# First attention of a four-stage block: ScalarE and VectorE take the order of the source

## The chip, the cores and the metric

One core of a Trainium2 chip runs the whole program. The core has five engines with a queue each: TensorE (PE: matrix products; PEld is its weight load), VectorE (DVE), ScalarE (ACT), GpSimd (POOL) and SyncE (SP, which issues most DMAs). An engine takes its queue in order: an instruction that waits for a semaphore holds up all behind it. Matrix products write to PSUM, eight banks of 128 partitions by 512 fp32 numbers. The metric is the device time of one execution in microseconds (us), as the median of three runs.

## The reference

The input x is 4 sequences (batches) of 512 tokens with 512 channels. Four layers are added to it in turn, each of a normed x: an attention, a feed-forward with ternary weights, a state-space scan and an attention with a mixture of experts. The change lies in the first, cut here to what is computed (16 heads of 32 channels; queries and keys are rotated, then divided by their root mean square, and the softmax is causal):

```python
def attention0(x, W_qkv, W_o):                 # x: (4, 512, 512), layer-normed
    qkv = einsum('btc,oc->bto', x, W_qkv).reshape(B, T, 3, 16, 32)
    q, k, v = (transpose(qkv[:, :, i], (0, 2, 1, 3)) for i in range(3))
    q = rms_norm(q * cos + rotate_half(q) * sin)
    k = rms_norm(k * cos + rotate_half(k) * sin)
    scores = where(causal, einsum('bhqd,bhkd->bhqk', q, k) / sqrt(32), -1e9)
    out = einsum('bhqk,bhkd->bhqd', softmax(scores), v)
    return out.transpose(0, 2, 1, 3).reshape(B, T, C) @ W_o.T

def ternary_quant(w):                          # for w1, w3 (1365 x 512) and w2 (512 x 1365)
    s = mean(abs(w))
    return clip(round(w / s), -1, 1) * s
```

The ternary weights are needed only in the second layer. The kernel prepares w1 and w3, and the scale of w2, while the first attention runs.

## The kernel before

**Order.** The program is written with a scheduler that works out each engine's order at compile time from a cost model, hands out buffers, and places all semaphores. The first attention stands in a block in which TensorE is ordered by hand, that is, as the source has it (`tc.manual_schedule(engines={mybir.EngineType.PE})`). VectorE, ScalarE and GpSimd are ordered by the scheduler there, so an instruction of a later line may pass one of an earlier line where the cost model expects it to be ready sooner.

**Buffers.** Four PSUM banks (`bank`) serve everything of one bank: projections `pq`, transposes `tp`, the products `av` and `sm`, the output projection `y`, and `sp`. A new one waits until the last reader of the bank's former tile is through. The other four banks are two pairs (`pair`) for the scores. Normed rows (`row`) have two buffers, as have rotations and their squares (one tag, `rot`), and the raw weight pieces (`q_w`).

**Prologue.** Batch 0 is normed (`norm`: statistics of four row tiles of 128 tokens, the factor by a power on GpSimd, L102 and L103). `turn_in` makes each normed row (L123, VectorE), transposes it on TensorE (L132) and copies it to `hT` on ScalarE (L133). `project(b, t, s)` (L284) computes queries (s=0), keys (1) or values (2) of row tile t. For queries and keys it then rotates: two products with the sine (L296) and one with the cosine (L300) on VectorE, their sum on GpSimd (L303), the square on ScalarE (L305), the sum of squares on VectorE (L306). Values are copied by ScalarE (L289). `scale_heads(b, i)` works out 1/rms for two row tiles by eleven short VectorE instructions (L312 to L323) and scales the heads (L325, two of 128x1024). `turn_heads(b, t)` transposes queries and keys (L132) and ScalarE copies them to `qkT` (L133). At the end of the prologue batch 1 is normed and its rows are transposed.

**Batches.** `attend(b, between)` goes through 16 steps m, four groups of four heads by four key tiles j. A step computes scores of 128 keys against the 512 - 128 j queries that see them (L359, two PSUM pairs of two heads), their exponentials on ScalarE (`pt`, L364, one instruction for each pair), and the causal cut on GpSimd (L365). Then it runs what `between[m]` holds, and last `weigh` of the step before: products with the values and with ones (`av` and `sm`, L377). After the fourth key tile of a group come VectorE's reciprocal of the sums (L385, 3.36 us) and the product with it (`oT`, L386).

`between` weaves other work in: `back` of the batch before (steps 1 to 4; output projection L340, sum L343), the projections of the next batch (step 0 and steps 5 to 15, in the order (0,0), (0,1), (1,0), (1,1), (0,2), (2,0), (2,1), (1,2), (3,0), (3,1), (2,2), (3,2) of (t, s)), `scale_heads` at 9 and 14, `turn_heads` at 12 and 13, and the weight pieces. After the last step follow `turn_heads` for tiles 2 and 3, and `norm` and `turn_in` of the batch after the next.

**Weight pieces.** `jobs` is a list of 43 pieces, each fetched by SyncE into `q_w` (L218); the end of a piece's job issues the load two places on. Eight pieces of w1 are measured in batch 0 (ScalarE: absolute value with a running sum, L234), eight quantized in batch 1 (VectorE, L201 and L202) in turn with pieces of w2 that are measured (L252). Batch 2 measures the last of w2 and w3, batch 3 quantizes w3. `find_scale` turns a weight's measured sums into its scale: `ternary_scale` sums them on VectorE (L187), adds up the partitions on TensorE (`sp`, L189) and makes three constants on VectorE (L193).

Of the kernel before, what the change touches and what calls it, by code (L numbers as in the profile page):

```python
# [19 lines left out]
P = 128  # L20
# [26 lines left out]
def block_kernel(ctx: ExitStack, tc: tile.TileContext, a: dict, out: bass.AP):  # L47
# [116 lines left out]
    with tc.tile_pool(name="a_w", bufs=1) as aw, tc.tile_pool(name="a_1", bufs=1) as a1, tc.tile_pool(  # L164
# [19 lines left out]
        def ternary_scale(pool, parts, name):  # L184

            tot = pool.tile([P, 1], F32, tag="q_tot", name="q_tot")
            nc.vector.tensor_reduce(tot, parts, AX.X, ALU.add)  # L187
# [68 lines left out]
        def find_scale(name):  # L256
            scales[name] = ternary_scale(a1, parts[name], name)
# [6 lines left out]
        normed, inputs_T, heads, squares, turned_qk, values, outs = {}, {}, {}, {}, {}, {}, {}  # L264

        def norm(b, pieces=1):
            normed[b] = []
            layer_norm(a1, xs[b], lambda t, op: normed[b].append(op), pieces)
            inputs_T[b] = a1.tile([P, NK, T], F32, tag="hT", name="hT")
# [4 lines left out]

        def turn_in(b, i):
            for t in (2 * i, 2 * i + 1):
                row = a2.tile([P, C], F32, tag="row", name="row")
                normed[b][t](row)
                transpose_into(inputs_T[b], row, t * P)
# [120 lines left out]
        with tc.manual_schedule(engines={mybir.EngineType.PE}):  # L400

            norm(0, 2)
            for i in range(2):
                turn_in(0, i)
                for t in (2 * i, 2 * i + 1):
                    project(0, t, 0)
                    project(0, t, 1)
                scale_heads(0, i)
# [5 lines left out]
            norm(1)  # L414
# [25 lines left out]
            for b in range(B):  # L440
# [1364 lines left out]
```

## Time and profile before

| | |
|---|---|
| Median of 3 runs | 1862.88 us (1862.3 to 1863.4) |
| The profiled execution | 1863.49 us, of which the span from first to last instruction is 1861.8 |
| PE busy | 1757.1 us, 94% of the span |
| DVE, ACT, POOL busy | 1123.3 (60%), 938.3 (50%), 568.4 us (31%) |
| Prologue, to the first scores | 0 to 63.4 us |
| Batch 0, 1, 2 (first scores to next first scores) | 88.0, 112.0, 96.5 us |
| Batch 3, to the end of its output projection | 67.9 us |
| All after the first attention | from 427.7 us |

A row of the order of time reads: start and length in us, engine, line and operation, the tile written and the tiles read, how many instructions are taken together, and in brackets how long the engine stood idle before and what released it. A row of busy time by stretch has the stretch, its length, the busy time of PE, PEld, DVE, ACT and POOL with the number of instructions, the clock granted to TensorE (1.00 is full), the DMA engines' busy share and GB/s. "x2" at a row with a wide shape can mean two instructions with their common length.

### The profile page before, as it was taken

Reading aid. Unit: us, or ns where it says so; the run is one execution under the profiler, and the core shown is the slowest. Engines: PE = TensorE matmul, PEld = TensorE weight load, DVE = VectorE, ACT = ScalarE, POOL = GpSimd, SP = SyncE. Lnnn points to the kernel's source line nnn. Section 1 sums busy time; section 2 is a strip of 40 time slices with the busy share of each in tenths; the row PEclk is TensorE's granted clock in tenths of the full one; section 3 lists DMA queues with packets and bytes.
Section 4 is the critical chain, followed back from the end, with each engine's and each line's share of the span. In section 5 each row is a group of like instructions: output and inputs, shape, how many; then the busy total and the mean of one; then the engine's idle time right before and its main releaser. Section 6 shows DMA issues by size and latency. Waiting matters only on the chain.

```text
span 1861.8 us, 27452 instructions
## 1 busy us (share of the span) xinstructions
PE 1757.1 (94%) x10374; PEld 1094.2 (59%) x10374; DVE 1123.3 (60%) x1812; ACT 938.3 (50%) x1940; POOL 568.4 (31%) x383
## 2 busy tenths in 40 slices
PE   7999999999999998899997989999999999999998
PEld 3434343436777766788886875656556554544444
DVE  6456545557656556999888886574766764222222
ACT  2433442332243526989989867675676652011111
POOL 3221212120112020889887860100000000244441
PEclk9999999999999999999999987999999999999999
DMA  7002300102001122323223200000010007455545
GB/s 245 20 1 72 104 1 1 29 18 71 10 28 43 57 80 68 103 94 104 57 63 112 58 28 1 1 24 1 1 35 24 24 24 246 132 91 91 91 80 141
DMA packets 74630, 115.07 MB, mean 62 GB/s; under 512 B 9546, under 2 KB 34762, under 8 KB 73940
## 3 DMA queue, kind: packets, MB, share of 16 engines
q1 hardware_dynamic: 64996, 90.87, 15.2%
q0 software_dynamic: 8656, 20.32, 6.1%
q8 instruction: 83, 1.36, 0.3%
q10 hardware_dynamic: 848, 2.13, 0.3%
q14 instruction: 47, 0.39, 0.1%
HBM read 83.02 MB, written 33.42 MB: 63 GB/s over the span
## 4 chain that ended last, share of the span: by engine, by line
PE 66%; ACT 10%; DVE 9%; issue 2%; DMA 2%; POOL 1%; DVEq 0%; ACTq 0%; POOLq 0%
PE pgr L1684 7%; PE pg L826 7%; PE ys L1135 4%; PE scd L1369 4%; PE yr L1705 4%; PE pq L284 3%; PE bu L1103 3%; PE y L1309 3%; PE y L844 3%; PE pge L1270 3%; PE bu L1098 3%; PE tpd L1392 2%; PE y L340 2%; ACT pr L1380 2%; PE tp L132 2%
## 5 line engine op out<-in xcount | busy, mean ns | idle before, releaser
L1122 POOL TENSOR_TENSOR hc<-h,cb 128x1024 f32<-128x1024 f32 x128 | 301.3, 2380 | 110.2 <-DVE h L1111 91.0
L1111 DVE TENSOR_TENSOR_SCAN h<-da,bu 128x512 f32<-128x512 f32 x256 | 294.9, 1203 | 24.6 <-PE bu L1103 10.5
L284 PE MATMUL pq<-wqkv,hT 128*128 128x512 f32 x384 | 179.6, 615 | 1.5 <-ACT hT L133 1.5
L1091 ACT ACTIVATE da<-delta_l,am 128x511 f32<-128x511 f32 x256 | 163.4, 709 | 2.4 <-DVE h L1111 2.4
L1380 ACT ACTIVATE pr<-scd,nm 128x128 f32<-128x128 f32 (+3 forms) x256 | 133.4, 531 | 57.4 <-DVE nm L1377 56.2
L826 PE MATMUL pg<-hTh,w 128*128 128x512 f32 (+1 forms) x352 | 146.2, 415 | 1.4 <-ACT hTh L813 0.7
L826 PE MATMUL pg<-hTl,w 128*128 128x512 f32 (+1 forms) x352 | 140.6, 400 | 0.2 <-DVE hTl L814 0.2
L1135 PE MATMUL ys<-ident,hc 128*128 128x128 f32 x1024 | 137.2, 278 | 3.2 <-DVE h L1111 1.4
L1103 PE MATMUL bu<-ident,bu 128*128 128x128 f32 x768 | 132.2, 279 | 7.8 <-ACT bu L1085 7.7
L1684 PE MATMUL pgr<-wgu,gTe 128*128 x304 | 137.1, 593 | 0.0
L1085 ACT ACTIVATE bu<-dxT,bts 128x512 f32<-128x512 f32 x192 | 124.4, 712 | 13.0 <-PE bu L1103 12.6
L284 PEld LDWEIGHTS pq<-wqkv,hT 128*128 128x128 f32 x384 | 71.5, 194 | 94.2 <-issue 84.8
L364 ACT ACTIVATE pt<-sc 128x1024 f32<-128x1024 f32 (+3 forms) x128 | 84.1, 698 | 83.5 <-PE sc L359 81.0
L1369 PE MATMUL scd<-kTd,qTd 32*128 32x512 f32 (+3 forms) x512 | 108.9, 505 | 14.4 <-ACT pr L1380 11.5
L1135 PEld LDWEIGHTS ys<-ident,hc 128*128 128x128 f32 x1024 | 119.3, 144 | 4.4 <-DVE h L1111 1.6
L1098 PE MATMUL bu<-diag_l,dxT 128*128 128x128 f32 x512 | 105.6, 289 | 14.0 <-DVE h L1111 10.3
L1377 DVE TENSOR_REDUCE nm<-scd 128x2 f32<-128x256 f32 (+3 forms) x128 | 105.0, 821 | 2.8
L1392 PE MATMUL tpd<-ident,pr 128*128 128x128 f32 x640 | 102.5, 291 | 2.7 <-ACT hTr L133 0.9
L1098 PEld LDWEIGHTS bu<-diag_l,dxT 128*128 128x128 f32 x512 | 81.7, 195 | 37.1 <-DVE h L1111 19.7
L365 POOL TENSOR_SCALAR_AFFINE_SELECT pt<-pt 128x512 f32<-128x512 f32 x64 | 43.5, 679 | 195.3 <-ACT pt L364 195.3
L1103 PEld LDWEIGHTS bu<-ident,bu 128*128 128x128 f32 x768 | 95.3, 145 | 12.0 <-ACT bu L1085 11.9
L1392 PEld LDWEIGHTS tpd<-ident,pr 128*128 128x128 f32 x640 | 75.3, 146 | 36.4 <-issue 23.0
(337 smaller groups left out, 3182.3 us busy)
## 6 DMA issues: line engine op xcount, KB each, us to landing
cb<-c_rows SPq DMA_DIRECT2D x64, 256.0 KB, 3.2
q_w<-in_w2T SPq DMA_DIRECT2D x20, 256.0 KB, 2.7
diag_l<-diags SPq DMA_DIRECT2D x64, 64.0 KB, 1.9
hrows<-h SPq DMA_DIRECT2D x4, 1024.0 KB, 4.3
acc<-x SPq DMA_DIRECT2D x16, 256.0 KB, 2.0
wgu<-in_r_gate SPq DMA_DIRECT2D x7, 512.0 KB, 9.3
wgu<-in_r_up SPq DMA_DIRECT2D x7, 512.0 KB, 10.0
wdn<-in_r_down SPq DMA_DIRECT2D x7, 512.0 KB, 9.4
```

The lines of the kernel that those rows point to most:

```text
L284: nc.tensor.matmul(y, inputs_T[b][:, k, t * P : (t + 1) * P], wqkv[:, k, s * C : (s + 1) * C], start=k == 0, stop=k == NK - 1,)
L826: nc.tensor.matmul(pg[:rows, i, :], w[:, k, f * P : f * P + rows], part[:, k, :], start=k + m == 0, stop=k + m == NK,)
L1091: nc.scalar.activation(da[:, k, 1:], delta[:, k, 1:], AF.Exp, scale=am[:, k, n : n + 1])
L1098: nc.tensor.matmul(bu[:, :P], loaded[b][1][:, 0, k * P : (k + 1) * P], scaled[b, n][0], start=True, stop=True,)
L1103: nc.tensor.transpose(bu[:, t * P : (t + 1) * P], scaled[b, n][t][:, k * P : (k + 1) * P], ident)
L1111: nc.vector.tensor_tensor_scan(h[:, i, :], decays[b, n][:, 2 * half + i, :], bu, 0.0, ALU.mult, ALU.add)
L1122: nc.gpsimd.tensor_tensor(hc, states.pop((b, n, half)), weighed[b, n].unsqueeze(1).to_broadcast([P, 2, T]), ALU.mult)
L1135: nc.tensor.matmul(sums[b][t][:, k * P : (k + 1) * P], hc[:, i, t * P : (t + 1) * P], ident, is_transpose=True, start=n == 0 and k == 0, s ...
L1369: nc.tensor.matmul(sc[:, i, :w], qT[at, g, t * P : w], kT[at, g, :w], start=True, stop=True)
L1380: nc.scalar.activation(pr[:, i, :w], sc[:, i, :w], AF.Exp, bias=nm[:, i : i + 1], accum_out=sums[b, g][:, t, 2 * p + i : 2 * p + i + 1],)
L1392: nc.tensor.transpose(tp[:, j * P : (j + 1) * P], pr[:, i, j * P : (j + 1) * P], ident)
L1684: nc.tensor.matmul(pg, gT[:, k, :], wgu[:, bass.ds(e, 1), k, :].rearrange("p e o -> p (e o)"), start=k == 0, stop=k == NK - 1,)
```

## The change

ScalarE and VectorE join TensorE in the hand-ordered block, so that within the first attention their order is that of the source. GpSimd and SyncE stay with the scheduler. The source is rearranged at four places:

- `norm` is cut in two. `measure_rows` (statistics and factor) of batch b+2 goes to step 11 of batch b; `make_room` (buffers) stays after the batch.
- `turn_in` is cut into `make_row` (VectorE) and `turn_row` (TensorE and ScalarE). Rows 0 and 1 of batch b+2 are made at step 15, rows 2 and 3 after the transposes of rows 0 and 1. In the prologue, rows 2 and 3 of batch 0 are made before the first rotations.
- The sum of a weight's measurements (`total_of`) stays at its step; the product with ones and the constants (`find_scale`) come one step later.
- As a consequence of the order alone, the weight pieces run at the steps at which the source has them, a square stands ahead of ScalarE's work of later lines, and the reductions, reciprocals and scalings follow each other as written.

```diff
+        totals = {}
+
+        def total_of(name):
+            totals[name] = a1.tile([P, 1], F32, tag="q_tot", name="q_tot")
+            nc.vector.tensor_reduce(totals[name], parts[name], AX.X, ALU.add)
+
+        def ternary_scale(name):
+
+            tot = totals[name]
             sp = bank("sp")
...
-        def norm(b, pieces=1):
+        def measure_rows(b, pieces=1):
             normed[b] = []
             layer_norm(a1, xs[b], lambda t, op: normed[b].append(op), pieces)
+
+        def make_room(b):
             inputs_T[b] = a1.tile([P, NK, T], F32, tag="hT", name="hT")
...
+        def make_row(b, t):
+            normed_rows[b, t] = a2.tile([P, C], F32, tag="row", name="row")
+            normed[b][t](normed_rows[b, t])
+
+        def turn_row(b, t):
+            transpose_into(inputs_T[b], normed_rows.pop((b, t)), t * P)
+
         def turn_in(b, i):
             for t in (2 * i, 2 * i + 1):
-                row = a2.tile([P, C], F32, tag="row", name="row")
-                normed[b][t](row)
-                transpose_into(inputs_T[b], row, t * P)
+                make_row(b, t)
+            for t in (2 * i, 2 * i + 1):
+                turn_row(b, t)
...
-        with tc.manual_schedule(engines={mybir.EngineType.PE}):
-
-            norm(0, 2)
+        engines = {getattr(mybir.EngineType, e) for e in ("PE", "DVE", "Activation")}
+        with tc.manual_schedule(engines=engines):
+
+            measure_rows(0, 2)
+            make_room(0)
             for i in range(2):
-                turn_in(0, i)
+                if i == 0:
+                    turn_in(0, 0)
+                    make_row(0, 2)
+                    make_row(0, 3)
+                else:
+                    turn_row(0, 2)
+                    turn_row(0, 3)
...
-            norm(1)
+            measure_rows(1)
+            make_room(1)
...
                     if (b, m) in scale_at:
-                        between[m].append(do(find_scale, scale_at[b, m]))
+                        between[m].append(do(total_of, scale_at[b, m]))
+                    if (b, m - 1) in scale_at:
+                        between[m].append(do(find_scale, scale_at[b, m - 1]))
...
+                if b + 2 < B:
+                    between[11].append(do(measure_rows, b + 2))
+                    for t in range(2):
+                        between[15].append(do(make_row, b + 2, t))
                 attend(b, between)
...
                 if b + 2 < B:
-                    norm(b + 2)
-                    turn_in(b + 2, 0)
-                    turn_in(b + 2, 1)
+                    make_room(b + 2)
+                    for t in range(NT):
+                        turn_row(b + 2, t)
+                        if t + 2 < NT:
+                            make_row(b + 2, t + 2)
```

More of the change, by code (lines that the diff above doesn't have):

```diff
@@ L182, in block_kernel @@
             nc.sync.dma_start(xs[b], by_tokens(a["x"], b))
-        def ternary_scale(pool, parts, name):
-            tot = pool.tile([P, 1], F32, tag="q_tot", name="q_tot")
-            nc.vector.tensor_reduce(tot, parts, AX.X, ALU.add)
+        totals = {}
[4 more added lines that the diff above has]
+            tot = totals[name]
             sp = bank("sp")
@@ L256, in find_scale @@
         def find_scale(name):
-            scales[name] = ternary_scale(a1, parts[name], name)
+            scales[name] = ternary_scale(name)
         scales = {}
         w1 = place("w1")
-        normed, inputs_T, heads, squares, turned_qk, values, outs = {}, {}, {}, {}, {}, {}, {}
-        def norm(b, pieces=1):
+        normed_rows, normed, inputs_T, heads, squares, turned_qk, values, outs = {}, {}, {}, {}, {}, {}, {}, {}
+        def measure_rows(b, pieces=1):
             normed[b] = []
             layer_norm(a1, xs[b], lambda t, op: normed[b].append(op), pieces)
+        def make_room(b):
             inputs_T[b] = a1.tile([P, NK, T], F32, tag="hT", name="hT")
```

## The prediction

> **What bounds the kernel now.** I read the engine shares first (TensorE busy 94% of the span), then busy time and granted clock by stage, then what TensorE waited for in each stage, then the order of time around each wait. All that the diff touches lies in the first attention, up to 427.7 us, so the stages are its prologue (to the first scores), batches 0 to 3, and the rest. Columns: stretch, length, busy time of PE, PEld, DVE, ACT, POOL, granted clock, DMA.
>
> ```profile
> 0.00:63.37 63.37, 50.88 (x161) 26.15 (x161) 39.95 (x93) 22.87 (x46) 15.55 (x20) 1.00 0.57 194
> 63.37:151.38 88.01, 83.37 (x529) 34.55 (x528) 47.44 (x80) 34.60 (x57) 22.38 (x25) 1.00 0.00 1
> 151.38:263.38 112.00, 104.11 (x564) 42.94 (x563) 63.88 (x107) 46.94 (x92) 22.19 (x25) 0.95 0.25 73
> 263.38:359.84 96.46, 93.93 (x547) 38.43 (x546) 43.95 (x73) 32.24 (x53) 21.18 (x24) 1.00 0.00 1
> 359.84:427.70 67.86, 63.60 (x451) 24.49 (x452) 42.89 (x58) 21.44 (x33) 12.23 (x18) 1.00 0.11 32
> ```
>
> TensorE is the bound everywhere, so only its pauses can be won or added. Batch 1 is the odd one: it lasts 112.0 us, while batch 2, whose TensorE work is the same but for four transposed rows at its end, takes 96.5. Where batch 1 loses is in its order of time:
>
> ```profile
> 179.90 0.63 ACT L252 ACTIVATE q_w<-q_w 128x512 f32<-128x512 f32 x1 [3.81 <-DMA q_w<-in_w2T]
> ...
> 180.53 1.92 ACT L364 ACTIVATE pt<-sc 128x1024 f32<-128x1024 f32 x2
> ...
> 181.58 1.83 PE L359 MATMUL sc<-qkT 32*128 32x384 f32 x8 [2.92 <-ACT pt L364]
> ...
> 183.34 5.40 PE L284 MATMUL pq<-wqkv,hT 128*128 128x512 f32 x8
> ```
>
> ScalarE stands at a weight piece that has not landed (3.81), the exponentials behind it are late, and the next scores wait 2.92 for their PSUM pair. Then a projection takes 5.40 where others take 3.70, since the clock is halved after each of the two pauses (2.92, then 2.83 at 210.84 plus 0.33):
>
> ```profile
> 183.90:187.30 3.40, 3.40 (x6) 1.33 (x5) 3.36 (x4) 2.12 (x4) 0.57 (x1) 0.50 0.32 67
> ...
> 211.20:218.00 6.80, 6.47 (x13) 2.35 (x10) 6.49 (x12) 3.89 (x8) 2.13 (x2) 0.50 0.40 127
> ```
>
> So pauses cost batch 1 6.1 us, and the clock half of 3.4 + 6.8 = 5.1. Pauses of 0.9 to 1.5 us in this stage leave the clock at 1.00.
>
> The unit of what follows is a rotation, the chain behind one projected piece over three engines. Its five rows in batch 2:
>
> ```profile
> 295.13 0.76 DVE L296 TENSOR_TENSOR rot<-pq,sin 128x256 f32<-128x256 f32 x2 [0.44 <-PE pq L284]
> ...
> 295.80 0.68 DVE L300 TENSOR_TENSOR qk<-pq,cos 128x512 f32<-128x512 f32 x1
> ...
> 296.57 1.27 POOL L303 TENSOR_TENSOR qk<-qk,rot 128x512 f32<-128x512 f32 x1 [2.81 <-DVE qk L300]
> ...
> 297.87 0.63 ACT L305 ACTIVATE sqk<-qk 128x512 f32<-128x512 f32 x1 [4.87 <-POOL qk L303]
> ...
> 298.53 0.69 DVE L306 TENSOR_REDUCE qkss<-sqk 128x16 f32<-128x512 f32 x1 [2.05 <-ACT sqk L305]
> ```
>
> From first to last it takes 4.09 us; the square ends 3.4 after the start. In source order, nothing on VectorE may pass between cosine and reduction, and nothing on ScalarE may pass a square that waits. A scaling (`scale_heads`) is 11 short instructions and two of 1.2: 5.5 us in batch 2 (310.87 to 316.40), 5.2 in the prologue.
>
> **Part 1, the prologue.** TensorE, whose order is the same, now waits longer for ScalarE. Before, the copies of the third and fourth normed row went ahead of the fourth square:
>
> ```profile
> 27.57 0.63 ACT L305 ACTIVATE sqk<-qk 128x512 f32<-128x512 f32 x1 [3.37 <-POOL qk L303]
> 28.10 1.07 ACT L133 ACTIVATE hT<-tp 128x512 f32<-128x512 f32 x2
> ```
>
> The source puts all four squares first. Rotations start at 16.13 and then every 4.09: 20.22, 24.31, 28.40. The fourth square ends 28.40 + 3.4 = 31.8, the copy (0.60) 32.4, and the next projection starts there and not at 28.73. TensorE's transposes before it ended at 27.3, so this pause is 5.1 us, and by the rows of batch 1 the clock will be halved for 3.4 to 6.8 us after it.
> VectorE: four rotations end 32.5, scaling 37.8, four more 54.2, scaling 59.5. Only then batch 1's statistics, which before filled gaps from 19.05 on: 4 x 0.84 = 3.4, the factor 0.2 and GpSimd's power 1.0 + 0.1, so its first row is ready at 64.8 (row 0.5).
> TensorE: four rotated projections and two values at 3.63 from 32.4 end 54.2 at full clock. The copies of the values stand behind the eighth square (50.2 + 3.4 = 53.6), ending 54.2 and 54.8; four transposes with ScalarE's copies let the next value projection start at 56.0, two of 3.63 end 63.3, four transposes 65.05, two rows 66.15, the other two wait for row buffers and VectorE and end 67.3. The first scores start there instead of 63.37: +3.9. Half clock adds 1.7 (3.4 us at half) or 3.4 (6.8 us), since from 54.2 on TensorE's own sum binds. Bounds +3.9 and +7.3; I take the middle spell, +5.6.
>
> **Part 2, weight pieces at their own steps.** All 43 loads stay on SyncE's queue in the same sequence; each is issued when the piece two jobs earlier is done, so one or two steps of 5 to 6 us ahead, and a piece lands in 2.9 to 3.5 us (rows at 171.69 and 197.26). ScalarE's waits for DMA in batch 1 go, with both pauses and both clock spells: -11.2. The pieces of w1, which before ran in the prologue, now put 0.96 each (0.77 + 0.19) into batch 0: two fall in steps 1 to 4, where ScalarE is the pacer (a pause of 0.91 and one of 0.60 there now). Walking those steps with exponentials of 1.94, 1.51, 1.08 and 0.66: the square after step 0 ahead of step 1's exponentials makes scores 2 end 0.7 later, the two pieces leave 0.4 at step 5. Batch 0: +0.4. Elsewhere a step has 3.63 of projection that covers a piece.
>
> **Part 3, reciprocal before scaling.** Batches 0 and 2 pause 1.4 us at step 9, because VectorE took the scaling first and the reciprocal of the group's sums after it:
>
> ```profile
> 316.40 3.35 DVE L385 RECIPROCAL r<-sm 128x512 f32<-128x512 f32 x1
> ...
> 319.80 1.06 PE L377 MATMUL sm<-pt,ones 128*32 128x512 f32 x8 [1.40 <-DVE r L385]
> ```
>
> In source order the reciprocal starts at 312.95, when its sums are done, and ends at 316.3: -1.4 in each. What is late next is the scaling, behind rotation 9: rotation 9 from 317.5 ends 321.6, scaling 327.1, and rotation 10, whose projection ended at 323.75, starts there.
>
> **Part 4, steps 10 to 14, the new waits.** A step's scores need the PSUM pairs that the exponentials of the step before free. Step 11's exponentials now stand behind rotation 10's square. In batch 2's times, without the 1.4: that square ends 327.1 + 3.4 = 330.5, the w3 piece at this step 331.5, the exponentials 331.9 and 332.25; TensorE wants scores 12 at 330.2. Pause 1.7, so this part takes the 1.4 back. In batch 0 no piece stands there: 0.75 to 1.1. In batch 1 a quantized piece (0.58 + 0.93) delays rotation 10 to 328.6; square 332.0, a w2 piece (0.82) 332.8, exponentials 333.2: pause 3.0.
> Step 12: the second transpose of `turn_heads` now waits for the cosine (tile freed by VectorE), 1.0 instead of 0.69; projection 13 waits for the qkT copy behind square 12, 0.3. In batch 1 rotation 12 also waits for batch 3's statistics (4 x 0.84), about as long as the pause has already made it late.
> Step 14: rotation 13 stands behind reduction 12, reciprocal (3.36) and oT (0.69): it starts 344.9, its square ends 348.3, the copy after it 348.9, and projection 14 starts 348.95 instead of 346.60. So batch 2 is +2.35 at that point; batch 0, with 0.7 less at step 12, +1.35; batch 1 +3.7 against batch 2's 346.60.
>
> **Part 5, the rest.** Rows 0 and 1 made ahead of the reciprocal cost nothing and win nothing: rows 2 and 3 still stand behind it and oT, and the last row (150.20 now) moves by 0.2. The scale's sum and product are 0.16 and 3 x 0.1, a step apart; VectorE has 4 us to spare there. GpSimd's powers move to step 11, where it idles some 5 us (5.31 ahead of 334.98). If that cover went, each would cost its 1.0. In batch 3 the w3 pieces go from steps 0 to 4 to every second step (1.5 us of VectorE, which has 9.6 us per group against 4.05 of reciprocal and oT): nothing, and the last ends before the 11.4 us of `back`.
>
> **The sum.** Prologue +5.6. Batch 0: 0.4 + 1.35 + 0.25 (rows, small waits) = +2.0. Batch 1: batch 2 up to its last transposes is 93.8, batch 1 is 106.4; 93.8 + 3.7 - 106.4 = -8.9, rows +0.2, and its pause of 3.0 is like the two that halved the clock: +1.7 if it does, +1.3 as I take it, so -7.4. Batch 2: +2.45. Batch 3 and later: 0. Together +2.7. The profiled execution took 1863.5 (span 1861.8 and 1.7 around it); this is within 0.6 of the median, so on the median 1862.9 + 2.7 = 1865.6.
> On the clock the rows say: 1.5 us of pause leaves it, 2.8 halves it. The Trainium skill, "TensorE: Matmul & The Clock Gate", section "What's actually happening", says the clock falls to half after an idle window of about 3.4 us that runs freely. By that rule alone the 3.0 of batch 1 need not halve it, and the sum would be +1.4; the 2.83 above speaks for the rows.
>
> **Rivals.**
> (a) Cancelled: no clock spell follows either new pause. Then +3.9 + 2.0 - 8.7 + 2.45 = -0.3, 1862.6. For it: where a pause falls in the gate's window is chance. Against: 5.1 us is longer than any pause that kept the clock.
> (b) Slower: the waits of Part 4 are worse. The clock drops after the clustered pauses of batches 0 and 2 too (1.7 each), and longest in the prologue (+7.3) and batch 1 (-8.7 + 3.4): 7.3 + 3.7 - 5.3 + 4.15 = +9.8, 1872.7. It decides when pauses of 1.7 and 1.0 within 8 us count as one of 2.8.
> (c) Faster: Part 4 costs nothing, because step 10's square is done before 330.2, that is, if VectorE reaches rotation 10 by 326.5 instead of 327.1 to 328.6 and the pieces on ScalarE fall after the exponentials. Then batch 0 is -0.7, batch 1 -13.5, batch 2 -1.2, prologue +5.6: -9.8, 1853.1. Against: the queue order puts piece and square first.
>
> **How the numbers follow.** Forecast (1863 to 1868.5) 0.55, (a) 0.17, (b) 0.20, (c) 0.08. Within 0.2%, 3.7 us and about what a measurement can tell from no change, is 1859.2 to 1866.6: all of (a) and, as its middle lies 1.0 below that bound, 0.57 of the forecast's share: 0.17 + 0.31 = 0.48. Slower is the rest of the forecast and (b), 0.44; faster is (c), 0.08. The range leaves out most of (c) and the far end of (b): 1860.5 to 1872.
>
> **What would show it.** Right: first scores at 67 to 71 us, TensorE pausing about 5 us at 27 with a half clock after it; batch 1 some 104 to 106 us long with no ScalarE wait on q_w above 0.5; scores waiting for exponentials at step 12, longest in batch 1; no wait of sums on the reciprocal at step 9. Wrong: a prologue of 63 to 65 (some copy passes the squares), or batch 1 near 98 (c) or above 108.

## The result, and the profile after

The changed kernel takes 1870.89 us (median of 16 runs, 1864.07 to 1873.92) against 1862.49 us before (16 runs, 1860.05 to 1865.03): a ratio of 1.0038, with a 95% interval of 1.0030 to 1.0046. It is slower by some 7 us by this ratio, and the two medians lie 8.4 us apart. The profiled execution took 1867.32 us, its span 1865.6, so it lies at the quick end of the runs, 3.6 us under their median. A second profile of the same kernel, taken for the experiments, has a span of 1871.1 and lies nearer to the middle.

Busy time and granted clock by stage come first, as before the change. The columns are stretch, length, busy time of PE, PEld, DVE, ACT and POOL, clock, and the DMA engines' share and GB/s. The stretches are the prologue, batches 0 to 2, and batch 3 up to the first product of the second layer (432.27 us before).

```profile
0.00:68.34 68.34, 52.86 (x160) 27.09 (x160) 36.44 (x86) 15.98 (x28) 15.29 (x20) 0.95 0.38 135
68.34:159.87 91.53, 85.19 (x529) 35.10 (x528) 47.36 (x79) 39.24 (x73) 21.41 (x25) 0.98 0.11 31
159.87:262.74 102.87, 96.60 (x564) 40.35 (x563) 62.33 (x104) 38.46 (x73) 22.61 (x25) 1.00 0.18 48
262.74:363.50 100.76, 95.92 (x548) 38.76 (x547) 43.86 (x73) 39.45 (x76) 20.36 (x24) 0.98 0.12 36
363.50:436.32 72.82, 65.68 (x467) 26.18 (x467) 50.03 (x77) 23.79 (x37) 13.24 (x19) 1.00 0.15 40
```

Against the profile before, the prologue is 5.0 us longer, batch 0 3.5 longer, batch 1 9.1 shorter, batch 2 4.3 longer, batch 3 0.4 longer: +4.1 us at 436.32. What follows takes as long as before. The one clock reading below 1.00 (batch 1, 0.95) has moved: batch 1 is now at full clock, and the prologue, batch 0 and batch 2 are not.

What TensorE waited for up to 440 us (total, times, longest) names the new pauses. The first line is mostly the start: 10.5 us pass before there is any row.

```profile
PE tp L132 <- DVE row L123: 12.7, 4, 10.5
PE sc L373 <- ACT pt L378: 7.9, 7, 2.6
PE pq L298 <- ACT hT L133: 4.7, 1, 4.7
PE tp L132 <- DVE qk L314: 3.5, 3, 1.2
PE pq L298 <- ACT qkT L133: 3.2, 6, 0.7
PE sp L194 <- DVE q_tot L188: 2.2, 1, 2.2
```

The prologue in order of time: the copies to `hT` stand behind the fourth square, the square behind the sum on GpSimd, and the projection behind the copies.

```profile
30.02 1.26 POOL L317 TENSOR_TENSOR qk<-qk,rot 128x512 f32<-128x512 f32 x1 [2.72 <-DVE qk L314]
31.32 0.63 ACT L319 ACTIVATE sqk<-qk 128x512 f32<-128x512 f32 x1 [3.35 <-POOL qk L317]
31.85 1.07 ACT L133 ACTIVATE hT<-tp 128x512 f32<-128x512 f32 x2
...
32.48 2.08 PE L298 MATMUL pq<-wqkv,hT 128*128 128x512 f32 x2 [4.72 <-ACT hT L133]
```

The clock is halved from within this pause on. Of these 6.83 us, TensorE worked in 4.97:

```profile
30.62:37.45 6.83, 4.97 (x6) 2.19 (x7) 5.06 (x14) 1.60 (x3) 0.66 (x1) 0.50 0.00 0
```

Batch 0 at step 2: the exponentials stand behind a square, and the scores wait for them.

```profile
75.98 0.63 ACT L319 ACTIVATE sqk<-qk 128x512 f32<-128x512 f32 x1 [4.53 <-POOL qk L317]
76.52 1.49 ACT L378 ACTIVATE pt<-sc 128x768 f32<-128x768 f32 x2
...
77.36 1.63 PE L373 MATMUL sc<-qkT 32*128 32x256 f32 x8 [1.54 <-ACT pt L378]
```

Batch 1 at steps 11 and 12, the same pattern once more: ScalarE was idle for 9.21 us for the sum, did its square and a weight piece, and only then the exponentials that the next scores need.

```profile
226.47 1.26 POOL L317 TENSOR_TENSOR qk<-qk,rot 128x512 f32<-128x512 f32 x1 [7.09 <-DVE qk L314]
227.77 0.63 ACT L319 ACTIVATE sqk<-qk 128x512 f32<-128x512 f32 x1 [9.21 <-POOL qk L317]
228.30 0.61 ACT L257 ACTIVATE q_w<-q_w 128x512 f32<-128x512 f32 x1
...
228.82 0.19 ACT L257 ACTIVATION_READ_ACCUMULATOR q_w<-q_w 128x1 f32 x1
228.91 0.64 ACT L378 ACTIVATE pt<-sc 128x256 f32<-128x256 f32 x2
...
229.33 1.40 PE L373 MATMUL sc<-qkT 32*128 32x512 f32 x8 [2.60 <-ACT pt L378]
```

And batch 2, where something else is late first: the sum of w2's measurements stands behind the reduction of rotation 10 on VectorE, and TensorE stands at its product with ones.

```profile
329.64 0.69 DVE L320 TENSOR_REDUCE qkss<-sqk 128x16 f32<-128x512 f32 x1 [2.04 <-ACT sqk L319]
...
330.25 0.15 DVE L188 TENSOR_REDUCE q_tot<-q_w 128x1 f32<-128x11 f32 x1
...
330.55 0.35 PE L194 MATMUL sp<-q_tot,ones 128*128 128x1 f32 x2 [2.16 <-DVE q_tot L188]
```

The waits on the other side of the account are gone: in batch 1 ScalarE no longer waits for any weight to land (2.92 and 2.83 us of TensorE's pauses before), and no sums wait for the reciprocal at step 9 (1.4 us each in batches 0 and 2 before). One wait of ScalarE at a weight piece is left in batch 1, 3.24 us at 176.25, but for VectorE and not for a load.

### The profile page after: what moved, and what is told of

It is laid out like the page before. It is cut to its first block, busy times and chain, and to the rows that moved or that the text cites. A ratio compares the mean times of both kernels' runs of the same rounds, so it can differ in the third digit from the quotient of the medians.

```text
span 1865.6 us, 27439 instructions
## 1 busy us (share of the span) xinstructions
PE 1753.0 (94%) x10374; PEld 1093.0 (59%) x10374; DVE 1122.1 (60%) x1812; ACT 935.3 (50%) x1940; POOL 566.3 (30%) x383
## 3 DMA queue, kind: packets, MB, share of 16 engines
q8 instruction: 83, 1.36, 0.3%
## 4 chain that ended last, share of the span: by engine, by line
PE 72%; DVE 11%; ACT 10%; issue 3%; POOL 2%; DMA 1%; SPq 0%; DVEq 0%; ACTq 0%; POOLq 0%
PE pq L298 7%; PE pgr L1715 7%; PE pg L857 7%; PE ys L1166 4%; PE scd L1400 4%; PE yr L1736 4%; PE bu L1134 3%; PE y L1340 3%; PE y L875 3%; PE y L354 3%; PE pge L1301 3%; PE bu L1129 3%; PE tpd L1423 3%; PE sc L373 2%; PE tp L132 2%
## 5 line engine op out<-in xcount | busy, mean ns | idle before, releaser
L1142 DVE TENSOR_TENSOR_SCAN h<-da,bu 128x512 f32<-128x512 f32 x256 | 295.2, 1204 | 26.5 <-PE bu L1134 10.2
```

What stands on the lines that cost most here:

```text
L1142: nc.vector.tensor_tensor_scan(h[:, i, :], decays[b, n][:, 2 * half + i, :], bu, 0.0, ALU.mult, ALU.add)
```

## The experiments

The theory T: a gain and a loss of about equal size, both from the orders of ScalarE and VectorE. The gain is the weight pieces, which come when their data is there. The loss is what queues behind a square or a reduction that itself waits for GpSimd. Every half-clock stretch that a pause sets off comes on top. The rivals are named with each run. The table gives the stages of the profiles that the text uses (us from first scores to first scores, and after "at" the clock where it is not 1.00); "total" is the time of the second layer's first product.

| Kernel | Prologue | Batch 0 | Batch 1 | Batch 2 | Batch 3 | Total | Median, ratio to before |
|---|---|---|---|---|---|---|---|
| before | 63.37 | 88.01 | 112.00 at 0.95 | 96.46 | 72.43 | 432.27 | 1862.49 |
| changed | 68.34 at 0.95 | 91.53 at 0.98 | 102.87 | 100.76 at 0.98 | 72.82 | 436.32 | 1870.89, 1.0038 |
| changed, again | 68.10 at 0.95 | 91.60 at 0.98 | 105.80 at 0.97 | 100.73 at 0.98 | 74.48 at 0.97 | 440.71 | 1872.75, 1.0048 |
| squares later, first stage only | 61.75 | 91.62 at 0.98 | 104.41 at 0.98 | 99.12 | 73.41 | 430.31 | 1861.34, 1.0005 |
| squares later | 61.36 | 86.36 | 102.31 at 0.98 | 96.51 at 0.98 | 72.60 | 419.14 | 1847.66, 0.9927 |
| and ahead of values' copies | 62.13 | 85.12 | 97.99 | 94.86 | 72.61 | 412.71 | 1841.13, 0.9900 |
| the same, PE ordered only | 61.25 | 86.54 | 107.84 at 0.98 | 96.47 | 74.68 at 0.98 | 426.78 | 1855.34, 0.9973 |

The times of before on the chips of the experiments are 1859.4 to 1861.2 us, so ratios are compared, not medians.

**1. Only TensorE in the source's order.**

```diff
-        engines = {getattr(mybir.EngineType, e) for e in ("PE", "DVE", "Activation")}
+        engines = {getattr(mybir.EngineType, e) for e in ("PE",)}
```

> The source of the changed kernel (its rows, its split of the scales' sum and product, its measuring of rows in step 11), with only TensorE kept in the source's order; ScalarE and VectorE go back to the scheduler. Theory T (the orders of ScalarE and VectorE make both the gains and the losses): the 4.72 us wait for the row copies in the prologue goes, first scores at 63 to 64 us; batch 1 goes back to 110 to 112.5 us with waits of 2 to 3 us for weights at ScalarE; the waits of the scores for the exponentials at step 12 are under 1 us; 1862 to 1865 us. Rival R (the rearranged source by itself costs the time): first scores still at 67 us or later, batch 1 at 103 us, 1867 us or more.

Measured: 1858.79 us, ratio 0.9985 (0.9974 to 0.9995). First scores at 63.23 us; ScalarE's longest wait for a piece of w2 is 5.2 us. R falls: the rearranged source by itself does not cost the time, it even gains a little. T's number for batch 1 was too high: it takes 106.60 us, not 110 to 112.5. One pause of 2.29 us is left there of the two.

**2 and 3. TensorE and one of the two other engines.**

```diff
+        engines = {getattr(mybir.EngineType, e) for e in ("PE", "DVE")}
```

> The changed kernel with TensorE and VectorE in the source's order and ScalarE left to the scheduler. T says that the prologue's wait comes from ScalarE's order (the copies of rows 2 and 3 stand behind the fourth square), so first scores at 63 to 65 us; the waits for the exponentials at step 12 (ScalarE's order) are under 1 us, while the wait of 2.2 us of the scale's matmul for its sum in batch 2 (VectorE's order) and the 1.2 us of the second transpose at step 12 stay; whether ScalarE's waits for weights in batch 1 come back says which order removed them: by T ScalarE's, so 110 to 112 us there. 1862 to 1866 us. Rival R2 (VectorE's order alone makes the gain of batch 1): 103 to 105 us there, and 1852 to 1858 us.

Measured: 1864.16 us, ratio 1.0019 (1.0008 to 1.0029). First scores at 65.58 us, a little above T's range. The longest wait of scores for exponentials is 1.2 us (2.6 with both orders), and the 2.15 us of the scale's matmul stays: both as T has it. The second transpose at step 12, which T had at 1.2 us, waits 0.69 in batches 0 and 2, and in batch 1 it waits for ScalarE's copy, 3.89 us. ScalarE waits for w2 to land again, up to 2.9 us, so it is ScalarE's order that takes this wait out. Batch 1 takes 107.52 us, again less than the 110 to 112 expected of T. R2's 103 to 105 is not met either. The reciprocal's waits at step 9 are gone here.

```diff
+        engines = {getattr(mybir.EngineType, e) for e in ("PE", "Activation")}
```

> The changed kernel with TensorE and ScalarE in the source's order and VectorE left to the scheduler. T: the prologue's wait of 4.7 us stays (first scores at 67 to 69 us), the waits for the exponentials at step 12 stay (2.6 us in batch 1), batch 1 stays at 102 to 105 us, the scale's sum in batch 2 is no longer waited for: 1866 to 1870 us. R2: batch 1 back at 110 us or more, 1872 us or more.

Measured: 1866.25 us, ratio 1.0031 (1.0019 to 1.0043), as T expected. The prologue's wait is there (6.32 us, first scores at 68.18), no wait of ScalarE for weights to land in batch 1 (105.29 us long, where T had 102 to 105), none at the scale's matmul. With VectorE left to the scheduler the wait for the reciprocal at step 9 comes back, in all three batches. TensorE's order of time, batch 2:

```profile
317.70 1.07 PE L391 MATMUL av<-pt,v 128*32 128x512 f32 x8
320.16 1.06 PE L391 MATMUL sm<-pt,ones 128*32 128x512 f32 x8 [1.39 <-DVE r L399]
```

The scores' wait of step 12 is not there as T said it would be (longest 1.5 us, at step 2): it needs both orders.

**4. The copies of the prologue ahead of the fourth square.**

```diff
-                else:
-                    turn_row(0, 2)
-                    turn_row(0, 3)
                 for t in (2 * i, 2 * i + 1):
                     project(0, t, 0)
-                    project(0, t, 1)
+                    project(0, t, 1, [do(turn_row, 0, 2), do(turn_row, 0, 3)] if t == 1 else ())
```

The list given to `project` is run between the sum on GpSimd and the square.

> The changed kernel with one thing moved: in the first stage rows 2 and 3 of batch 0 are turned, and so copied by ScalarE, ahead of the fourth square instead of behind it. T: the 4.72 us wait at 27 to 32 us falls below 1 us, and with it the 6.8 us at half clock after it: first scores at 62 to 64 us instead of 68.3, the other batches as they are, so 1862 to 1866 us, 4 to 7 us under the changed kernel. Rival R3 (the wait is for something other than the square ahead of the copies, as the rows of VectorE or the transposes): first scores stay at 67 us or later, and the time at 1870 us.

Measured: 1866.35 us (1859.89 to 1874.61), ratio 1.0036 (1.0024 to 1.0048). The 4.72 us fell to 0.73, so the cause of that wait is shown. But first scores came at 65.79 us, not at 62 to 64, and the ratio is not to be told from the changed kernel's (1.0038). The last squares of the prologue did the same harm 20 us later:

```profile
49.65 0.52 PE L132 MATMUL tp<-ident,qk 128*128 128x128 f32 x3 [1.42 <-DVE qk L314]
52.13 1.12 PE L132 MATMUL tp<-ident,qk 128*128 128x128 f32 x8 [1.85 <-ACT v L303]
```

These are TensorE's transposes of the heads: one waits for a rotation that is late on VectorE, the other for the copies of the values, which stand behind the eighth square (50.88 us). A half-clock stretch of 3.41 us follows. R3 falls as it was put; that the whole prologue was one wait falls too.

**5. The squares and reductions one projection later.** This goes at the root instead of at one wait.

```diff
             nc.gpsimd.tensor_tensor(dst, dst, rot, ALU.add)
-            sq = a2.tile([P, H, D], F32, tag="rot", name="sqk")
-            nc.scalar.activation(sq, dst, AF.Square)
-            nc.vector.tensor_reduce(squares[b][:, t, s * H : (s + 1) * H], sq, AX.X, ALU.add)
+            squares_left()
+            left.append(do(square, dst, squares[b][:, t, s * H : (s + 1) * H]))
```

`squares_left` runs what the projection before left behind, and is also called after a copy of values; `square` holds the three lines taken out. In the prologue, `scale_heads(0, 0)` moves behind the first projection of row tile 2, and `scale_heads(0, 1)` behind the first two values. TensorE's order is the same.

> The changed kernel with the square of each rotated projection and its reduction put one projection later in the source (in the first stage the two scalings of the heads move behind them). T: the new waits have one root: ScalarE's square and VectorE's reduction stand directly behind a GpSimd sum, and hold both engines idle for 2 to 3.4 us per projection while other work queues behind them. So the copies in the prologue are no longer held (wait of 4.72 us below 1 us, first scores at 62.5 to 64.5 us), the scores of step 12 wait for the exponentials under 1 us in each batch (2.6 us in batch 1), the scale's matmul in batch 2 waits under 0.5 us (2.16 us), batch 1 takes 99 to 102 us, batch 2 97 to 98.5 us: 1854 to 1860 us, below both. Rival R4 (the orders as such are too tight, and the waits only move to the next neighbour, as the rotations or the transposes): pauses of the same sum elsewhere, and 1864 us or more.

Measured: 1847.66 us, ratio 0.9927 (0.9913 to 0.9940), more than T had claimed, and far from R4. The prologue's 4.72 us is a wait of 0.25, the scores of step 12 and the scale's matmul do not appear among TensorE's pauses of 0.5 us or more. How the idle time of the two engines went shows in their waits up to 440 us. First the changed kernel, VectorE and ScalarE:

```profile
DVE qkss L320 <- ACT sqk L319: 65.7, 32, 2.1
```

```profile
ACT sqk L319 <- POOL qk L317: 153.4, 32, 9.2
```

Then the kernel with the squares later:

```profile
DVE qkss L331 <- ACT sqk L330: 36.4, 10, 6.1
```

```profile
ACT sqk L330 <- POOL qk L318: 30.9, 12, 7.8
```

All 32 squares had made ScalarE wait, and all 32 reductions VectorE; now 12 and 10 do. In the kernel before the change, where the scheduler chose, it was 29 and 23:

```profile
DVE qkss L306 <- ACT sqk L305: 46.0, 23, 5.6
```

```profile
ACT sqk L305 <- POOL qk L303: 74.3, 29, 7.8
```

A new pause came, as R4 said, but only at the ends of batches 0 and 1: transposes wait 2.22 and 3.68 us for normed rows. T had not seen it.

**6. w1's pieces off steps 1 and 3, on top of that.**

```diff
-            at_step = {(0, 1 + 2 * n): n for n in range(2 * NK)}
+            at_step = {(0, m): n for n, m in enumerate((5, 7, 8, 9, 11, 13, 14, 15))}
```

> As the kernel with the squares one projection later, and the measuring of w1's pieces of batch 0 moved off steps 1 and 3 (to steps 5, 7, 8, 9, 11, 13, 14, 15). T: the wait of 1.54 us of step 2's scores for the exponentials comes from the piece in step 1, which ScalarE does ahead of them; it falls below 1 us, batch 0 gets 0.6 us shorter, and 1.7 us more where the pause had halved the clock. In the later steps of batch 0 ScalarE has time, by 42 us idle of 90. So 0.5 to 2.5 us under that kernel. Rival: the pieces hold the squares and copies of the later steps instead, and the time is the same or up to 2 us longer.

Measured: 1849.55 us, ratio 0.9940 (0.9927 to 0.9952): no gain beside 0.9927. Batch 0 is 86.36 us in both. T was wrong here: the wait of step 2's scores (1.54 us) does not come from the piece. It had gone with the square of step 0, which had stood ahead of step 1's exponentials. Run 7, with the pieces off these steps and the squares in place, has it unchanged (1.54).

**7. The neighbours moved, the squares left in place.**

```diff
-                    between[9].append(do(scale_heads, n, 0))
+                    between[10].append(do(scale_heads, n, 0))
...
-            scale_at = {(1, 0): "w1", (2, 10): "w2", (3, 0): "w3"}
+            scale_at = {(1, 0): "w1", (2, 6): "w2", (3, 0): "w3"}
...
-                    between[11].append(do(measure_rows, b + 2))
+                    between[3].append(do(measure_rows, b + 2))
...
-                    between[12].append(do(turn_heads, n, 0))
-                    between[13].append(do(turn_heads, n, 1))
+                        if m in (13, 14):
+                            between[m].append(do(turn_heads, n, m - 13))
```

With these go the edits of 4 and 6.

> The other way to the same end: the squares stay where the changed kernel has them, and what stands around them is moved: in the prologue the copies of rows 2 and 3 ahead of the fourth square, w1's pieces off steps 1 and 3, the first scaling of the heads from step 9 to 10, the measuring of rows from step 11 to 3, w2's sum from step 10 to 6, the turning of the heads' first two rows one step later. T: the wait at the scale's matmul (2.16 us) and that of the scores at step 12 (2.6 us in batch 1) go below 1 us; the prologue stays at 65 to 66 us, since the transposes of the heads wait for the values' copies behind the last squares; batch 0 88.5 to 89.5 us, batch 1 99 to 101.5 us, batch 2 96.5 to 98 us: 1855 to 1861 us. Rival R4 as before: the pauses reappear at other steps, 1864 us or more.

Measured: 1874.19 us, ratio 1.0075 (1.0063 to 1.0087), no better than the changed kernel on the same chip (1.0048, run 8) and rather slower. The two waits that it aimed at are gone, and longer ones have come: in its profile, projections wait for the copies to `qkT` that free their bank, 15.4 us in six pauses of 1.47 to 3.71. The one in batch 1:

```profile
237.07 1.09 PE L132 MATMUL tp<-ident,qk 128*128 128x128 f32 x8
241.74 4.11 PE L298 MATMUL pq<-wqkv,hT 128*128 128x512 f32 x5 [3.57 <-ACT qkT L133]
```

For this set of moves R4 holds. Moving what queues behind a blocked instruction only chose another to wait.

**8. The changed kernel again.**

> The changed kernel once more, unaltered, timed beside the other variants, and with a second profile. Where its half-clock stretches fall is the question. In the first profile they begin on a grid of 3.41 us, and nearly always right after a piece of that grid in which TensorE was busy for less than some 55%. If that is the rule (theory G), a pause of 1.5 to 3 us halves the clock in one execution and not in another, by how the grid cuts it: the pauses of the first profile come back at the same steps with the same lengths, only the pause of 4.7 us in the prologue halves the clock in both profiles, and the single ones after step 2 of batch 0 and the scale's matmul of batch 2 need not; the stage times without the clock's share agree to 0.5 us with 64.9, 89.8, 102.9, 99.1. Rival F (the stretches belong to places of the program): the same three stretches at 31, 78 and 331 us. Time 1864 to 1872 us, 1.002 to 1.005 of before.

Measured: 1872.75 us, ratio 1.0048 (1.0031 to 1.0064). The pauses named above return at the same steps, with lengths equal to 0.02 us. The half-clock stretches do so in part: 31, 78.4 and 334.4 us (331 in the first profile) are there again, as rival F says, and two are new: one at 402.7 in batch 3, and one of 6.83 us at 228.6 in batch 1, where the first profile has none behind the same pause. For G, TensorE's busy time is taken in pieces of 3.41 us that end 0.5 us before a point of the grid. The lines of the first profile come in pairs: the piece with the pause of 1.54 us and the half-clock stretch after it, the two pieces that share the pause of 2.60, and the piece with the pause of 2.16 and the stretch after it.

```profile
74.51:77.92 3.41, 1.87 (x20) 0.43 (x8) 0.69 (x1) 1.94 (x4) 1.27 (x1) 1.00 0.00 0
78.42:81.83 3.41, 3.41 (x24) 0.78 (x24) 0.00 (x0) 1.32 (x4) 0.94 (x2) 0.50 0.37 107
224.69:228.10 3.41, 2.04 (x19) 0.61 (x17) 1.70 (x4) 0.33 (x1) 1.26 (x1) 1.00 0.33 102
228.10:231.52 3.42, 2.19 (x10) 1.06 (x11) 3.02 (x6) 2.88 (x8) 1.37 (x1) 1.00 0.25 77
327.10:330.51 3.41, 1.29 (x4) 0.22 (x2) 1.26 (x3) 1.53 (x4) 1.26 (x1) 1.00 0.00 0
331.01:334.42 3.41, 3.41 (x24) 0.95 (x16) 0.21 (x3) 0.37 (x1) 0.63 (x1) 0.50 0.38 107
```

Then the second profile at the pause of 2.60 (2.62 there):

```profile
224.69:228.10 3.41, 1.86 (x19) 0.45 (x17) 1.54 (x4) 0.49 (x1) 1.26 (x1) 1.00 0.29 102
228.60:235.43 6.83, 6.26 (x13) 2.62 (x14) 5.00 (x12) 3.21 (x7) 2.91 (x3) 0.50 0.28 90
```

In the first profile the pause of 2.60 us is shared by two pieces, busy 2.04 and 2.19: 60 and 64%. In the second it lies some 0.2 us earlier against the grid, the first piece is busy 1.86, 55%, and the clock is halved after that. This is as G has it, but by a narrow margin. Over the fourteen profiles, 151 half-clock stretches begin after the prologue's first products. All lie on such a grid; ahead of 131 of them TensorE was busy below 56% in the 3.41 us that ended 0.5 us before. Ahead of 20 it was not (74% at the stretch at 402.7), and 31 other pieces below 56% were followed by none. The 56% and the 0.5 us were fitted to these same data, so this is a rule of thumb.

Other kernels that keep these pauses speak against F. Run 4 has all three at the same steps (1.54, 2.61 and 2.15 us), and its batches 0 to 2 run at full clock:

```profile
65.79:156.01 90.22, 83.67 (x530) 34.87 (x529) 47.54 (x79) 39.24 (x73) 21.39 (x25) 1.00 0.10 31
156.01:258.90 102.89, 96.60 (x564) 40.34 (x563) 62.34 (x104) 38.47 (x73) 22.66 (x25) 1.00 0.16 48
258.90:358.01 99.11, 94.28 (x547) 38.38 (x546) 43.84 (x73) 39.45 (x76) 20.40 (x24) 1.00 0.12 37
```

**9. The square ahead of the values' copy.** At the ends of batches 0 and 1 the last square stood behind a copy that waits for TensorE.

```diff
             if s == 2:
+                squares_left()
                 nc.scalar.copy(values[b][:, t, :], y)
-                squares_left()
                 return
```

> The kernel with the squares one projection later, and one thing more: where the next projection is one of values, the square goes ahead of its copy on ScalarE and not behind it. In the profile without this, the reduction of the last square waits at the end of batches 0 and 1 (idle 6.13 and 4.02 us for the square, which stands behind a copy that waits for TensorE), the scaling of the heads and two rows follow, the reciprocal of 3.35 us comes after the rows at 142.05 and 244.34 us, and the transposes of the rows 2 and 3 wait 2.22 and 3.68 us behind it. T: the reduction starts 3 to 4 us sooner, so the reciprocal starts when its sums end, and the waits fall to 1 us each, with the half-clock stretch after each gone: 3 to 7 us under that kernel, 1840 to 1846 us. Rival: the reciprocal's own 3.35 us is what the rows wait for, whenever the square comes: the waits stay within 0.5 us, and the time within 2 us.

Measured: 1841.13 us (1839.54 to 1845.81), ratio 0.9900 (0.9882 to 0.9918). Both pauses for rows are 0.99 us, and no half-clock stretch is left in the first 636 us. TensorE's waits up to 440 us, the largest of this profile:

```profile
PE tp L132 <- DVE row L123: 11.5, 4, 9.3
PE tp L132 <- ACT qkT L133: 3.2, 8, 0.7
PE sc L384 <- ACT pt L389: 3.0, 4, 1.2
```

Of the 11.5 us, 9.3 are the start, before there is any row. T holds, its rival falls.

**10. Four rows ahead of the reciprocal, on top of that.**

```diff
-                    for t in range(2):
+                    for t in range(NT):
                         between[15].append(do(make_row, b + 2, t))
...
-                        if t + 2 < NT:
-                            make_row(b + 2, t + 2)
...
+            if b > 1 and t > 1:
+                normed_rows[b, t] = a2.tile([P, H, D], F32, tag="rot", name="row").rearrange(
...
```

> The same, and rows 2 and 3 of batches 2 and 3 are made in step 15 too, ahead of the reciprocal, in two buffers that the rotations leave free by then. T: no transpose of a row waits for VectorE at the ends of batches 0 and 1 any more (2.22 and 3.68 us with the squares later alone); these batches at 84 to 85 us and 97 to 99 us, 1838 to 1844 us. Rival: the buffers of the rotations come free too late or the first rotation of the next batch waits for them, and the time is that of the run beside it or more.

Measured: 1841.94 us, ratio 0.9903 (0.9885 to 0.9920). The last pauses for rows went, and the first layer ends 0.5 us sooner in the profile (412.24); in time it is not to be told from the run beside it.

**11. The squares later in the prologue only.**

```diff
             left.append(do(square, dst, squares[b][:, t, s * H : (s + 1) * H]))
+            if b > 0:
+                squares_left()
```

In this stage the square also goes ahead of the values' copy, as in run 9.

> The changed kernel with the squares one projection later in the first stage alone; in the batches they stand as in the changed kernel. It prices the two parts of the loss apart. T: first scores at 61 to 62.5 us instead of 68.3, with no half-clock stretch at 31 us; the batches keep their waits (2.6 us of the scores at step 12 in batch 1, 1.2 us of the second transpose, 2.2 us of the scale's matmul in batch 2): 91, 103 to 106 and 99 to 101 us; 1863 to 1867 us, some 6 us under the changed kernel. Rival: the first stage's wait is worth less, since the batches give it back, and the time stays within 2 us of 1871.

Measured: 1861.34 us (1858.27 to 1866.76), ratio 1.0005 (0.9992 to 1.0017). First scores at 61.75 us; the batches keep their waits (2.60, 1.17 and 2.16 us). The time is a little below T's range. With the prologue's pause the ratio is 1.0038 or 1.0048, without it 1.0005, so the loss against before goes with that pause. Here the prologue is 1.6 us shorter than before; what the four batches lose and win cancels in this profile (368.6 us together, against 368.9). The other squares later (run 5) then take 0.8% more.

**12. The best source with only TensorE ordered.**

```diff
-        engines = {getattr(mybir.EngineType, e) for e in ("PE", "DVE", "Activation")}
+        engines = {getattr(mybir.EngineType, e) for e in ("PE",)}
```

> The kernel of 1841 us (squares one projection later and ahead of the values' copies) with only TensorE in the source's order, ScalarE and VectorE left to the scheduler. It tells whether that gain needs the orders of these two engines, or is the better source alone. T: the scheduler moves the work by its own estimates, so the waits of batch 1 for weights and exponentials of 2 to 3 us come back: batch 1 104 to 108 us, 1852 to 1860 us. Rival: the scheduler finds as good an order, 1840 to 1846 us.

Measured: 1855.34 us, ratio 0.9973 (0.9962 to 0.9984), as T has it. Batch 1 takes 107.84 us with a pause of 2.75 for exponentials, and ScalarE waits for w2 again (up to 4.7 us). So the orders of ScalarE and VectorE are worth 0.7% with a source fit for them: 0.9900 against 0.9973.

## Why the prediction was right, and where it was not

The forecast of 1865.6 us was too low by 5.3, inside its range. "Within 0.2%" had a little more chance than "slower", and it is slower.

- **Part 1, prologue, +5.6.** Right in place and cause; that the size came out, +5.0, is in part luck. The pause is 4.72 us where 5.1 was said, the half clock 6.83 us where 3.4 to 6.8 was said, the first scores at 68.34 against 67 to 71. Run 4 shows the cause of the pause, run 11 its price in time: with the prologue's squares later the ratio falls from 1.0038 (1.0048 in the second comparison) to 1.0005, 6 to 8 us. But two terms of the sum were off and offset each other. At full clock six projections in a row take 20.87 us, 3.45 each, and not 3.63, which is 1.5 us over the eight after the pause. And the half clock costs 2.45 us (23.32 against 20.87) where 1.7 was counted. The rows, before and after:

```profile
28.73 20.87 PE L284 MATMUL pq<-wqkv,hT 128*128 128x512 f32 x48 [1.47 <-ACT hT L133]
```

```profile
32.48 23.32 PE L298 MATMUL pq<-wqkv,hT 128*128 128x512 f32 x48 [4.72 <-ACT hT L133]
```

- **Part 2, weight pieces, -11.2.** Right that ScalarE's waits for loads go (the 3.24 us for VectorE were not foreseen: it had said none above 0.5); runs 1 to 3 show that it is ScalarE's order that does it. The batch was said to be 104 to 106 us long and is 102.87 and 105.80 in the two profiles. The 5.1 us of clock in this term are no certain gain, though: the second profile pays 3.4 of them again (6.83 us at half).
- **Part 3, the reciprocal, -1.4 twice.** Right: no such wait with VectorE in the source's order, 1.36 to 2.35 us in all three batches without it (run 3).
- **Part 4, steps 10 to 14.** The mechanism is right in each step that it names, most sizes within 0.4 us. Scores 12 wait 0.54 in batch 0 (said 0.75 to 1.1) and 2.60 in batch 1 (3.0); the second transpose 1.17 (1.0); projection 13 0.35 (0.3). In batch 2 the same late rotation 10 hits another instruction first: the scale's matmul waits 2.16 us where the scores were to wait 1.7.
- **Part 5, the rest, nil.** Wrong in "VectorE has 4 us to spare there": the sum of w2's measurements is short, 0.15 us, but it stands behind a reduction that waits, and at 330.25 us had nothing to spare at all. Also wrong by a little at the rows: they wait 0.99 us against 0.34 before, where +0.2 was counted. Only what stands ahead of an instruction in its queue tells when it runs, not the idle share of the engine.
- **The clock.** This is the step that was wrong: "1.5 us of pause leaves it, 2.8 halves it". A pause of 1.54 at step 2 of batch 0 and one of 2.16 in batch 2 were followed by 3.41 us at half clock in both profiles of the changed kernel, one of 2.60 in only one of them. In run 4 none of the three was, and in run 11 those of 1.54 and 2.60 were and that of 2.16 was not (batch 2 at full clock). The rows that left the clock alone were also misplaced: those of 0.91 to 1.47 us lie in the prologue and in batches 0 and 2, and batch 1 has none of that length. So the length of a pause does not decide; how the grid cuts it fits most cases (run 8), and why the others differ stays open. With the pauses of 1.54 and 2.16 (1.7 us of clock each) batches 0 and 2 are +3.5 and +4.3 and not +2.0 and +2.45. The Trainium skill ("TensorE: Matmul & The Clock Gate", section "What's actually happening") has a window of some 3.4 us that runs freely. The length agrees with these profiles (3.41), and all stretches of a profile lie on one grid; whether the grid is free of the program's start the runs leave open. The same section has the clock fall after an idle window. An idle window these profiles do not show: around the pauses of 1.54, 2.62 and 2.16 us the pieces before the stretches were 55, 55 and 38% busy.
- **The sum.** Taken apart, the forecast of +2.7 was +4.8 for work and waiting and -2.1 for the clock. Up to the second layer the two profiles have some +3.3 and +2.0 for work and waiting, and +0.8 and +6.4 for the clock. (The clock's cost is half of the time at half clock outside the prologue's pause: 11.8 and 23.0 us, against 10.2 before.) The waits were taken too long and the clock's cost too low, and the two misses partly cancel.
- **The rivals.** (b), 1872.7, came closest, by its own mechanism (clock stretches after the small pauses too) though not by its condition: no two pauses had to come together, a single one of 1.54 was followed by a stretch. (a) and (c) are out.

How the median comes to be 3.6 us over the profile: span times (1 - mean clock) is the time that the half clock cost at most, as TensorE also stood idle in some of it. It is rounded to 0.9 us, since the clock is given in thousandths. In the 7 runs of the second comparison its median is 44.9 us, against 36.3 for before; span times clock is 1826.4 against 1823.7. Of the 11.6 us between those medians, some 2.7 or more are work and waiting, and up to 8.6 the clock.

## What to carry to other kernels

An instruction that waits for another engine must not stand directly behind its producer in a queue that is kept in the source's order: put it one unit of work later, where its input has long been there. Removing that one fault, in two steps (runs 5 and 9), took out most of the small waits and turned +0.4% into -1.0%, whereas moving what queues behind it (run 7) only picked the next victim. Where a kernel runs at full clock, price each pause of 1.5 us or more with a chance of a half-clock stretch on top, and judge by several runs.

## What the runs showed of the hardware that was not expected

- The same program, its pauses as good as equal in two profiles, runs between 1863.84 and 1873.61 us (7 runs); its mean clock goes with the time, in the first 16 runs from 0.976 in the slowest to 0.981 in the quickest.
- Half-clock stretches come in multiples of 3.41 us on a grid, and a piece of the grid that is half busy can be followed by one. In the two profiles of the changed kernel the grid lies at the same times from the first instruction (stretches at 30.6 and 78.4 us in both), while the work lies 0.2 us earlier against it in the second (first scores at 68.34 and 68.10); that little may have added a stretch of 6.83 us. Whether the grid itself moves in other executions was not recorded. A kernel with few pauses loses less: 29.4 us (median of 5 runs) with the squares ahead of the values' copies, 44.9 with the changed kernel.
